# Queries of 16 of 32 head groups by seven products of quarters, and one buffer for query weights, in a float32 decoder kernel

## The chip, the cores and the metric

The kernel runs on one core of one Trainium2 chip. The metric is the device time of one execution in microseconds (us). Three runs of the kernel before took 1465.74 us in the median (1463.15 to 1471.24). The engines of the core are named as in the profile: PE multiplies matrices, PEld is its loading of weights, DVE and ACT work elementwise and along rows, POOL does some elementwise work and the indexed DMAs, SP issues DMAs. All data are float32.

## The reference: what is computed

Four batches of 512 rows of 512 values (x) go through two gated layers. Layer 0 is a small self-attention over a context and a linear layer whose weights are made of bits. Layer 1 is a cross-attention of 16 heads and a mixture of 16 experts, which works on batch 0 alone. The part that the change touches is the query of layer 1:

```python
q = (hidden_states @ Wq).reshape(B, Sq, H, D)      # 512 wide in, 16 heads of 128
k = (encoder_hidden_states @ Wk).reshape(B, Skv, H, D)
v = (encoder_hidden_states @ Wv).reshape(B, Skv, H, D)
q = rmsnorm(q, gq)
k = rmsnorm(k, gk)
scores = jnp.einsum('bqhd,bkhd->bhqk', q, k) * scale
attn = jax.nn.softmax(scores, axis=-1)
out = jnp.einsum('bhqk,bkhd->bqhd', attn, v)
return out.reshape(B, Sq, H * D) @ Wo
```

## The kernel before

**Groups and steps.** Layer 1 works in 32 groups: batch b (4) by pair of heads g (8), `groups[m]`. One step is one head, i = 0 to 63, with m, h = divmod(i, 2); h is 0 in an even step and 1 in an odd one. `step(i)` (L1187) issues four quarters. Each starts with one tile of scores (L856: 128 queries by 512 keys, into one of two psS banks), followed by pieces of other work so that PE always has something to do.

**What lies in a step.** In an even step: keys and values of the next group (`keys_values`, L733, eight matmuls of 512 columns, two quarters), then the values product of the head two steps back (`values`, L903, third quarter), then half of the output projection of the group two back (`project`, L954, fourth quarter). In an odd step: the queries of the next group (`queries`, L807, one head in the first quarter and one in the second), `values`, and the other half of a projection.

**Queries.** `queries(m, h)` multiplies the 128 columns of the weights of head h by `lx1[b]`, the normalised and transposed rows of the batch, in four matmuls of 512 columns into one of three psA banks. ACT squares the result into `sq` (L813) and copies it, scaled, into `qT` (L815). After the second head, `part` on DVE sums the squares in blocks (L827), `total` on PE adds over partitions (L835), and `scale` makes 1/rms on DVE (L840 to L843) and POOL (the power at L192). The exponential of the scores needs it.

**Scores to probabilities.** For each tile of scores: DVE takes the maximum (L864) and multiplies it (L866), ACT takes the exponential (L873), DVE divides (L877, L878) and transposes blocks (L260). After a head's fourth tile SP moves the blocks across partitions with 16 DMAs (L268, `big<-tP`), into one of two buffers that `values` reads.

**The keys' way.** POOL scales the keys (L759), DVE transposes blocks (L770), and ACT issues one DMA out and four back (L777, L785, `kT<-k_d`).

**Order.** All work is issued in an order written out by hand: `tick()` counts matmuls, `later(n, f)` issues f when n more were counted, and `put(i, quarter, f)` adds f to a quarter of a step. Engines run their instructions in that order.

**Weights.** `load_wq` (L708), `load_wkv` (L142) and `load_wo` (L714) are issued by SP. Each has two buffers. `load_wq(m + 2)` is issued in the second quarter of the even step of group m.

**Experts.** From step 22 to step 55, 17 blocks of 128 gathered rows take two steps each: transposes (L1021), two products of 352 columns (`hidden`, L1029), the gate on ACT and DVE (L1038, L1039, L1043), transposes (L1048), a product down (`down`, L1057), a copy to `y` (L1065) and its DMA out. From step 57 on, 16 gathers on POOL (L1104) bring these rows back and DVE adds them to x (L275), four a step, each ten ticks after its gather. Four times in the kernel the rows of a batch are normalised and transposed for the queries (`turned_rows`, L226, L244, L249).

Of the kernel before, what the change touches and what calls it, by code (L numbers as in the profile page):

```python
# [9 lines left out]
F32 = mybir.dt.float32  # L10
# [21 lines left out]
FCH = [(0, 128), (128, 128), (256, 96)]  # L32
NSLOT = 2 * NE - 1
SPILL = 1
TB = 32
# [19 lines left out]
def tile_gated_decoder(  # L55
# [31 lines left out]
    def ps_a():  # L87
        return ps("psA", 3)
# [16 lines left out]
    def row(tag, bufs):  # L105
        return work.tile([P, 512], F32, tag=tag, bufs=bufs, name=tag)

    def col(n, tag):
        return tiny.tile([P, n], F32, tag=tag, name=tag)

# [95 lines left out]
    def rows_stats(b):  # L206

        stats = {}

        def chunk(c):  # L210
            if c == 0:
                stats["mv"] = tiny.tile([P, NC, 2], F32, tag="mv", name="mv")
            st = col(6, "st")
            nc.vector.bn_stats(st, x_sb[:, b * NC + c, :])
            nc.vector.bn_aggr(stats["mv"][:, c, :], st)
            if c == NC - 1:
                ve = col(NC, "ve")
                nc.vector.tensor_scalar(ve, stats["mv"][:, :, 1], EPS, None, ALU.add)
                stats["rs"] = col(NC, "rs")
                rsqrt(stats["rs"], ve, NC)  # L220

        return [lambda c=c: chunk(c) for c in range(NC)], stats

    def normalised(b, c, mv, rs):
        xn = row("xn", 2)
        nc.vector.tensor_scalar(  # L226
            xn, x_sb[:, b * NC + c, :], mv[:, c, 0:1], rs[:, c : c + 1], ALU.subtract, ALU.mult
        )
        return xn
# [96 lines left out]
    def l0_stats(b):  # L326

        pieces, stats = rows_stats(b)

        def gates():  # L330
            gate0[b] = gr = col(NC, "gr")
            nc.vector.tensor_scalar(gr, stats["rs"], tg[:, 0:1], None, ALU.mult)
            gm = col(NC, "gm")
            nc.vector.scalar_tensor_tensor(gm, stats["mv"][:, :, 0], -1.0, gr, ALU.mult, ALU.mult)
            for c in range(NC):
                x_c = x_sb[:, b * NC + c, :]
                later(c, lambda x_c=x_c, c=c: nc.scalar.activation(
                    x_c, x_c, AF.Identity, bias=gm[:, c : c + 1]
                ))

        return pieces[:-1] + [lambda: (pieces[-1](), later(3, gates))]
# [75 lines left out]
    def layer0_attention():  # L417
# [57 lines left out]

        load_wq(0)
        load_wq(1)
        load_wo(0)
# [15 lines left out]
        for h in range(G):  # L494
            queries(0, h)
        linear(NB - 1, turned0[NB - 1], [0, 1])

# [19 lines left out]
    def route():  # L517
# [20 lines left out]

        zero = row("xg", 1)
        nc.gpsimd.memset(zero, 0.0)  # L540
# [10 lines left out]
        ef_b = ef.unsqueeze(1).broadcast_to(CE)  # L551
        hit = small_tile([P, TOPK, NC, NE], "hit")
        for k in range(TOPK):
# [103 lines left out]
    def bias_row():  # L657
# [23 lines left out]
        yield  # L681
        brow.append(row("y", 2))
        nc.vector.tensor_copy(brow[0], pb)
# [17 lines left out]
    wq_of, wo_of = {}, {}  # L701
    q_of, sq_of, rq_of, kn_of, k_of, v_of, o_of = {}, {}, {}, {}, {}, {}, {}
    turned, moved, ends = {}, {}, {}
    n_heads = G * len(groups)

    def load_wq(m):
        t = work.tile([P, KC, GD], F32, tag="wq", name="wq")
        nc.sync.dma_start(t, wq_v[:, :, cols(m)])  # L708
        wq_of[m] = t

# [6 lines left out]
    def keys_values(m, chunks):  # L717
# [32 lines left out]
        def scale():  # L750
            kss = col(NC * G, "kss")
            nc.vector.tensor_reduce(
                kss, st["sq"].rearrange("p c (h d) -> p (c h) d", h=G), AX.X, ALU.add
            )
            nc.vector.tensor_scalar(kss, kss, 1.0 / D, EPS, ALU.mult, ALU.add)
            rk = col(NC * G, "rk")
            rsqrt(rk, kss, NC * G)
            kn_v = kn.rearrange("p c (h d) -> p c h d", h=G)
            nc.gpsimd.tensor_tensor(  # L759
                kn_v, kn_v,  # L760
                rk.rearrange("p (c h) -> p c h", h=G).unsqueeze(3).broadcast_to([P, NC, G, D]),
                ALU.mult,
            )
# [33 lines left out]
    def queries(m, h):  # L797
# [21 lines left out]
        if h < G - 1:  # L819
            return  # L820
        n = G * S // TB
        st = {}

        def part():

            st["part"] = col(n, "part")
            nc.vector.tensor_reduce(  # L827
                st["part"], sq.rearrange("p h (j r) -> p (h j) r", r=TB), AX.X, ALU.add,
                apply_transpose=True,
            )  # L830
# [6 lines left out]
        def scale():  # L837

            own = col(n, "own")
            nc.vector.tensor_tensor(own, st["pq"][:, 0:n], mine, ALU.mult)  # L840
            v = col(G * NC, "qss")
            nc.vector.tensor_reduce(v, own.rearrange("p (c a) -> p c a", a=NT), AX.X, ALU.add)
            nc.vector.tensor_scalar(v, v, 1.0 / D, EPS, ALU.mult, ALU.add)  # L843
            rq_of[m] = col(G * NC, "rq")
            rsqrt(rq_of[m], v, G * NC)
# [319 lines left out]
    for c in range(NC):  # L1165
        for k in range(TOPK):
            put(last + 1 + c, k, lambda c=c, k=k: add_row(c, k))
    for b in range(1, NB):
        i = (b - 1) * NG * G + NG
        for j, f in enumerate(turned_rows(b, lx1, lnt)):  # L1170
            put(i + j // NC * (1 + j % NC), 3 if j >= NC else j, f)
        if b > 1:
            put(i, 3, lambda b=b: load_ctx(b))
# [13 lines left out]
    def step(i):  # L1187
        m, h = divmod(i, G)
        pieces = [[], [], [], []]
        if i >= G:  # L1190
            pieces[0 if i == n - 1 else 2].append(lambda: values(i - G))
        elif h > 0:
            pieces[3].append(lambda: tick(8))
        if i == n - 1:
# [7 lines left out]
        if h == 0:  # L1202
            if 0 < m < M - 1:
                pieces[0].append(lambda: keys_values(m + 1, [0, 1]))
                pieces[1].append(lambda: keys_values(m + 1, [2, 3]))
            if m + 2 < M:
                pieces[1].append(lambda: load_wq(m + 2))
                pieces[3].append(lambda: load_wkv(m + 2))
            if m >= 2:
                pieces[3].append(lambda: project(m - 2, [2, 3]))  # L1210
            if 2 <= m < M:
                pieces[3].append(lambda: later(4, lambda: load_wo(m)))
        elif i < n - 1:
            if m + 1 < M:
                pieces[0].append(lambda: queries(m + 1, 0))
                pieces[1].append(lambda: queries(m + 1, 1))
            if m >= 1:
                pieces[3].append(lambda: project(m - 1, [0, 1] if m < M else [0, 1, 2, 3]))
        for quarter in range(4):
            if i < n:  # L1220
                scores(i, quarter)
            for f in pieces[quarter] + extra.get((i, quarter), []):
                f()
# [73 lines left out]
```

## Time and profile before

| what | value |
|---|---|
| median of three runs | 1465.74 us |
| the profiled execution's own time | 1464.92 us |
| its span, first to last instruction | 1462.8 us |
| granted PE clock, mean | 0.993 |
| scores L856 on PE | 262.7 us, 512 instructions |
| keys and values L733 on PE | 231.9 us, 512 |
| queries L807 on PE | 231.3 us, 512 |
| values L903 on PE | 226.6 us, 504 |
| projection L954 on PE, three kinds of bank | 124.9 + 66.2 + 60.1 us |
| experts' hidden products L1029 on PE | 86.0 us, 272 |
| idle of PE before the projection, for ACT's oT (L910) | 11.0 us |

The page gives for each engine the time in which it was busy. Matmuls overlap, so a group's busy time over its count is not what one costs in a row; start to start is. Idle time of an engine counts only where another one waits for it: the views of waits name who ended a wait. Windows cut the span into stretches, since shares of the whole mix stages with different limits.

### The profile page before, as it was taken

The page shows a single profiled execution, that of the slowest core. Times are in us where ns is not written, and L with a number is a line of the kernel's source. Part 1 is how long each engine was busy: PE and PEld are TensorE (multiplying, and loading weights), DVE is VectorE, ACT ScalarE, POOL GpSimd, SP SyncE. Part 2 cuts the span into 40 slices and gives each one's busy share as a digit, 9 for nine tenths or more (in the row PEclk, how much of TensorE's full clock was granted, in tenths as well). Part 3 has the DMA queues.
Part 4 walks back from the last instruction along what each step waited for, and adds up shares of the span by engine and source line. Part 5 has one row for each costly group of instructions (what it writes and reads, how often), then busy time and mean ns, then how long its engine had stood idle before and what let it go on. Part 6 is the DMA issues. An engine that isn't in the chain of part 4 may idle for free.

```text
span 1462.8 us, 13699 instructions
## 1 busy us (share of the span) xinstructions
PE 1427.7 (98%) x3745; PEld 669.5 (46%) x3745; DVE 962.3 (66%) x2160; ACT 533.4 (36%) x1196; POOL 286.2 (20%) x210
## 2 busy tenths in 40 slices
PE   8999999999999999999999999999999999999898
PEld 4544444444444444444444444444444444444334
DVE  4778766677776776665655565665666556567784
ACT  4642233333443433334233333323433333333331
POOL 1324415323111111111111111111011111102310
PEclk9999999999999999999999999999999999999999
DMA  7424016545544545566556576556556656545642
GB/s 258 168 96 163 1 55 164 149 139 128 138 133 132 143 134 166 157 184 169 176 177 178 159 214 192 145 172 204 170 162 186 183 168 192 167 135 167 180 128 74
DMA packets 155346, 226.89 MB, mean 155 GB/s; under 512 B 24576, under 2 KB 90640, under 8 KB 155264
## 3 DMA queue, kind: packets, MB, share of 16 engines
q1 hardware_dynamic: 127312, 177.86, 41.7%
q10 hardware_dynamic: 23040, 33.56, 7.5%
q0 software_dynamic: 4912, 14.53, 3.5%
q8 instruction: 33, 0.54, 0.2%
q14 instruction: 49, 0.40, 0.1%
HBM read 129.62 MB, written 30.17 MB: 109 GB/s over the span
## 4 chain that ended last, share of the span: by engine, by line
PE 79%; DVE 10%; SPq 4%; ACT 3%; DMA 2%; issue 1%; POOL 0%; ACTq 0%; DVEq 0%; POOLq 0%
PE psA L733 13%; PE psS L856 12%; PE psA L807 12%; PE psO L903 11%; PE psA L954 6%; PE psA L1029 6%; PE psO L954 4%; SPq L268 4%; PE psT L954 3%; PE psA L1057 3%; PE psA L363 2%; DMA big<-tP 2%; ACT prob L873 2%; DVE tP L260 1%; PE psA L691 1%; DVE nmax L864 1%
## 5 line engine op out<-in xcount | busy, mean ns | idle before, releaser
L873 ACT ACTIVATE prob<-psS,sb,rq 128x512 f32<-128x512 f32 x256 | 199.2, 778 | 607.0 <-DVE sb L866 605.5
L856 PE MATMUL psS<-kT,qT 128*128 128x512 f32 x512 | 262.7, 596 | 2.2 <-ACT prob L873 1.1
L733 PE MATMUL psA<-wkv,ctx 128*128 128x512 f32 x512 | 231.9, 592 | 0.0
L807 PE MATMUL psA<-lnT,wq 128*128 128x512 f32 x512 | 231.3, 592 | 0.0
L903 PE MATMUL psO<-big,v 128*128 128x512 f32 x504 | 226.6, 592 | 0.0
L864 DVE TENSOR_REDUCE nmax<-psS 128x1 f32<-128x512 f32 x256 | 172.7, 675 | 30.7 <-PE psS L856 28.9
L877 DVE RECIPROCAL rden<-den 128x1 f32<-128x1 f32 x256 | 40.7, 159 | 224.5 <-ACT prob L873 223.2
L260 DVE STREAM_TRANSPOSE tP<-prob 128x512 f32<-128x512 f32 x252 | 179.1, 711 | 8.4 <-DVE prob L878 0.5
L807 PEld LDWEIGHTS psA<-lnT,wq 128*128 128x128 f32 x512 | 96.7, 190 | 118.6 <-issue 108.1
L903 PEld LDWEIGHTS psO<-big,v 128*128 128x128 f32 x504 | 95.8, 190 | 120.5 <-issue 112.6
L733 PEld LDWEIGHTS psA<-wkv,ctx 128*128 128x128 f32 x512 | 96.4, 190 | 118.8 <-issue 112.3
L192 POOL TENSOR_TENSOR rq<-qss,mhalf 128x8 f32<-128x8 f32 x32 | 53.2, 1661 | 493.5 <-DVE qss L843 493.4
L192 POOL TENSOR_TENSOR rk<-kss,mhalf 128x8 f32<-128x8 f32 x32 | 52.6, 1644 | 443.3 <-DVE rden L877 281.4
L878 DVE TENSOR_SCALAR prob<-prob,rden 128x512 f32<-128x512 f32 x256 | 133.1, 520 | 9.0
L954 PE MATMUL psA<-wo,oT 128*128 128x512 f32 x256 | 124.9, 606 | 11.1 <-ACT oT L910 11.0
L856 PEld LDWEIGHTS psS<-kT,qT 128*128 128x128 f32 x512 | 93.4, 191 | 91.6 <-issue 71.4
L1029 PE MATMUL psA<-gu,xgT 128*128 128x352 f32 x272 | 86.0, 459 | 0.0
L954 PEld LDWEIGHTS psA<-wo,oT 128*128 128x128 f32 x256 | 48.3, 192 | 74.5 <-issue 55.5
L770 DVE STREAM_TRANSPOSE tK<-kn 128x256 f32<-128x256 f32 x128 | 45.4, 412 | 39.1 <-POOL kn L759 39.1
L1029 PEld LDWEIGHTS psA<-gu,xgT 128*128 128x128 f32 x272 | 51.7, 190 | 37.9 <-issue 16.3
L954 PE MATMUL psO<-wo,oT 128*128 128x512 f32 x128 | 66.2, 643 | 0.0
L275 DVE SCALAR_TENSOR_TENSOR x_sb<-psA,tg,x_sb 128x512 f32<-128x512 f32 x80 | 57.9, 724 | 6.7 <-PE psA L691 3.8
(173 smaller groups left out, 1509.4 us busy)
## 6 DMA issues: line engine op xcount, KB each, us to landing
big<-tP SPq DMA_DIRECT2D x1008, 64.0 KB
k_d<-tK ACTq DMA_DIRECT2D x32, 512.0 KB
kT<-k_d ACTq DMA_DIRECT2D x128, 128.0 KB
wq<-in_wq_dram SPq DMA_DIRECT2D x32, 512.0 KB
wo<-in_wo_dram SPq DMA_DIRECT2D x32, 512.0 KB
gu<-in_gate_dram SPq DMA_DIRECT2D x16, 704.0 KB
gu<-in_up_dram SPq DMA_DIRECT2D x16, 704.0 KB
wkv<-in_wk_dram SPq DMA_DIRECT2D x32, 256.0 KB
```

The costliest lines, as they stand in the source:

```text
L192: nc.gpsimd.tensor_tensor(out, v, mhalf[:, :n], ALU.pow)
L260: nc.vector.transpose(tP[:, :, c, :], e.rearrange("p (j r) -> p j r", r=TB))
L268: nc.sync.dma_start(pT[t * TB : (t + 1) * TB, g].rearrange("r j q -> r (j q)"), tP[g * TB : (g + 1) * TB, t * NC : (t + 1) * NC].rearrange ...
L733: nc.tensor.matmul(pp, ctxs[b][:, k, c * P : (c + 1) * P], wkv[:, k, :, :].rearrange("p a n -> p (a n)"), start=(k == 0), stop=(k == CC - 1),)
L807: nc.tensor.matmul(pp, wq[:, k, h * D : (h + 1) * D], lx1[b][:, k, :], start=(k == 0), stop=(k == KC - 1))
L856: nc.tensor.matmul(sc, q_of[m][h][:, c * P : (c + 1) * P], k_of[m][:, :, h, :], start=True, stop=True)
L864: nc.vector.tensor_reduce(nmax, sc, AX.X, ALU.max, negate=True)
L873: nc.scalar.activation(e, x, AF.Exp, bias=sb, scale=scale, accum_out=st["den"])
L878: nc.vector.tensor_scalar(st["e"], st["e"], rden, None, ALU.mult)
L903: nc.tensor.matmul(po, v[:, k, h * D : (h + 1) * D], pT[:, :, k, :], start=(k == 0), stop=(k == NC - 1))
L954: nc.tensor.matmul(pp, oT[:, j, c * P : (c + 1) * P], wo[:, j, :], start=(j == 0), stop=(j == G - 1))
L1029: nc.tensor.matmul(st[a][:, :FF], st["xgT"][:, k * P : (k + 1) * P], st["gu"][:, a, k, :], start=(k == 0), stop=(k == KC - 1),)
```

## The change

For groups 12 to 27 (`SWITCH`) the queries of a group, a product of 256 weight columns (two heads) by 512 rows with 512 summed over, are cut into quarters: heads by halves of the sum by halves of the rows. Seven products of quarters, each two matmuls of 256 columns, take the place of eight such products (which are the eight matmuls of 512 columns). The sums and differences of quarters that they need are made by POOL for the weights (`combine`), once for each group, by DVE for the rows (`combine_rows`), once for each of three batches, and by ACT and DVE for the results (`second`, `fourth`, `upper`, `lower`). Four products are issued in the last quarter of the even step (part 0) and three in the second quarter of the odd step (part 1). They stay in two psA banks in between.

```diff
     def load_wq(m):
-        t = work.tile([P, KC, GD], F32, tag="wq", name="wq")
-        nc.sync.dma_start(t, wq_v[:, :, cols(m)])
-        wq_of[m] = t
+        w = work.tile([P, KC, GD], F32, tag="wq", bufs=1, name="wq")
+        nc.sync.dma_start(w, wq_v[:, :, cols(m)])
+        if not by_quarters(m):
+            wq_of[m] = w
+            return lambda: None
...
+        def combine():
+            s1, s2, s4 = (sums[:, j] for j in range(3))
+            s3 = quarter(1, 0)
+            nc.gpsimd.tensor_tensor(s1, quarter(1, 0), quarter(1, 1), ALU.add)
+            nc.gpsimd.tensor_tensor(s2, s1, quarter(0, 0), ALU.subtract)
+            nc.gpsimd.tensor_tensor(s3, quarter(0, 0), s3, ALU.subtract)
+            nc.gpsimd.tensor_tensor(s4, quarter(0, 1), s2, ALU.subtract)
+            wq_of[m] = [quarter(0, 0), quarter(0, 1), s4, quarter(1, 1), s1, s2, s3]
+
+        return combine
+
+    def combine_rows(b):
...
+        nc.vector.tensor_tensor(t3, quarter(1, 1), quarter(0, 1), ALU.subtract)
+        nc.vector.tensor_tensor(t1, quarter(0, 1), quarter(0, 0), ALU.subtract)
+        nc.vector.tensor_tensor(t2, quarter(1, 1), t1, ALU.subtract)
+        nc.vector.tensor_tensor(t4, quarter(1, 0), t2, ALU.subtract)
+        lxs_of[b] = [quarter(0, 0), quarter(1, 0), quarter(1, 1), t4, t1, t2, t3]
...
+    def quarter_queries(m, part):
+        ws, xs = wq_of[m], lxs_of[groups[m][0]]
+
+        def product(j, out, start):
+            for k in range(HK):
+                nc.tensor.matmul(
+                    out, ws[j][:, k, :], xs[j][:, k, :], start=start and k == 0, stop=k == HK - 1,
+                    skip_group_check=True,
+                )
+                tick(0.5)
+
+        if part == 0:
+            px, py = ps_a(), ps_a()
+            q_of[m] = q0, q1 = [row("qT", 3) for h in range(G)]
...
+            def second():
+                nc.scalar.copy(u2, px[:, 0:HS])
+                nc.vector.tensor_tensor(u2, px[:, HS:S], u2, ALU.add)
+
+            def fourth():
+                nc.vector.tensor_tensor(u3, py[:, 0:HS], u2, ALU.add)
+                nc.vector.tensor_tensor(q1[:, HS:S], py[:, HS:S], u3, ALU.add)
+
+            product(0, px[:, 0:HS], True)
+            product(5, px[:, HS:S], False)
+            later(0, second)
+            product(6, py[:, 0:HS], True)
+            product(4, py[:, HS:S], False)
+            later(0, fourth)
+            return
...
+        def upper():
+            nc.scalar.copy(q0[:, 0:HS], px[:, 0:HS])
+            nc.vector.tensor_tensor(q1[:, 0:HS], px[:, HS:S], u3, ALU.add)
+
+        def lower():
+            nc.vector.tensor_tensor(q0[:, HS:S], py[:, HS:S], u2, ALU.add)
+            for h in (1, 0):
+                nc.scalar.activation(sq[:, h, :], q_of[m][h], AF.Square)
+            for h in (0, 1):
+                nc.scalar.activation(q_of[m][h], q_of[m][h], AF.Identity, scale=gqk)
+
+        product(1, px[:, 0:HS], False)
+        product(3, px[:, HS:S], True)
+        later(0, upper)
+        product(2, py[:, HS:S], False)
+        later(0, lower)
+        square_sums(m, sq)
```

`square_sums` holds the old `part`, `total` and `scale` unchanged. In `step` (q is m + 1, late says that group q is made by quarters):

```diff
-            pieces[0 if i == n - 1 else 2].append(lambda: values(i - G))
+            pieces[0 if i == n - 1 or h and late else 2].append(lambda: values(i - G))
...
             if m + 2 < M:
-                pieces[1].append(lambda: load_wq(m + 2))
-                pieces[3].append(lambda: load_wkv(m + 2))
-            if m >= 2:
+                pieces[2 if late else 3].append(lambda: load_wkv(m + 2))
+            if m >= 2 and not late_before:
                 pieces[3].append(lambda: project(m - 2, [2, 3]))
...
+            if late and q < M:
+                pieces[3].append(lambda: quarter_queries(q, 0))
         elif i < n - 1:
...
+            if q < M:
+                pieces[1].append(lambda: (quarter_queries if late else queries)(q, 1))
+            if m + 2 < M:
+                pieces[2].append(lambda: later(6, load_wq(m + 2)))
+            if late:
+                pieces[2].append(lambda: project(m - 1, [0, 1]))
             if m >= 1:
-                pieces[3].append(lambda: project(m - 1, [0, 1] if m < M else [0, 1, 2, 3]))
+                pieces[3].append(lambda: project(m - 1, [2, 3] if late else [0, 1]))
+            if late and q < M:
+                pieces[3].append(lambda: later(2, lambda: load_wo(q)))
...
-            for f in pieces[quarter] + extra.get((i, quarter), []):
+            more = extra.get((i, quarter), [])
+            for f in more + pieces[quarter] if late and h and quarter == 2 else pieces[quarter] + more:
```

In words: in odd steps before a changed group the values product comes in the first quarter, both halves of a projection in the third and fourth, and the load of the next `wo` after them. For all groups the query weights are loaded in the third quarter of the odd step instead of the second of the even one, into the one buffer; before the first step, `load_wq(1)` is issued after the queries of group 0.

The rest makes room for `wqs` and `lxs`: most of the small column tiles get two or three buffers instead of eight, the normalised rows `xn` share the two buffers of `y`, `zero` uses the buffer of `xgT`, `brow` that of `xg`, and `hit` that of `tK`. And the 16 row additions at the end are spread three to a step:

```diff
-            put(last + 1 + c, k, lambda c=c, k=k: add_row(c, k))
+            put(last + 1 + (c * TOPK + k) // 3, (c * TOPK + k) % 3, lambda c=c, k=k: add_row(c, k))
     for b in range(1, NB):
...
+        if (b + 1) * NG > SWITCH[0]:
+            put(2 * max(b * NG, SWITCH[0]) - 2, 1, lambda b=b: combine_rows(b))
```

## The prediction

> **What bounds the kernel now.** First the page's engine table and its row of tenths, then the windows by stage, the waits of PE, and the timeline of one group amid the expert blocks.
>
> ```profile
> PE 1427.7 (98%) x3745; PEld 669.5 (46%) x3745; DVE 962.3 (66%) x2160; ACT 533.4 (36%) x1196; POOL 286.2 (20%) x210
> ```
>
> PE is busy for 98% of the span, but a busy PE need not be a paced one. The windows show where it is full (columns: stretch, length, then busy time and instructions of PE, PEld, DVE, ACT, POOL, the granted clock, DMA share, GB/s):
>
> ```profile
> 178.00:581.00 403.00, 396.20 (x947) 176.34 (x946) 285.98 (x628) 152.98 (x351) 90.42 (x65) 0.99 0.48 132
> ...
> 780.00:980.00 200.00, 200.00 (x524) 95.41 (x523) 120.21 (x273) 70.09 (x163) 30.16 (x19) 1.00 0.61 180
> ...
> 1300.00:1463.00 163.00, 148.55 (x376) 67.58 (x374) 110.48 (x229) 50.78 (x118) 31.26 (x25) 0.97 0.48 136
> ```
>
> From 581 to 1300 us, where the 17 expert blocks and the 16 changed groups lie, PE has no idle time and the waits of PE list nothing; DVE is busy 60%, ACT 35%, DMA 61%. So in that stretch time is what PE streams, and a microsecond less of matmul is a microsecond less of span as long as nothing else becomes late. The timeline gives the rate (start, length, engine, line, tiles, shape, count):
>
> ```profile
> 623.76 2.53 PE L1029 MATMUL psA<-gu,xgT 128*128 128x352 f32 x8
> 626.13 1.02 PE L856 MATMUL psS<-kT,qT 128*128 128x512 f32 x2
> ...
> 637.94 3.60 PE L807 MATMUL psA<-lnT,wq 128*128 128x512 f32 x8
> 641.37 0.49 PE L1048 MATMUL psT<-ident,hh 128*128 128x128 f32 x3
> ```
>
> ```profile
> 1444.98 1.06 PE L934 MATMUL psA<-big,v 128*128 128x128 f32 x8
> 1445.87 0.60 PE L924 MATMUL psT<-ident,prob 128*128 128x128 f32 x4
> ```
>
> Lengths contain an overlapping tail, so I read from start to start. Each matmul of the program is two instructions (x8 for four). 512 columns: (641.37-637.94)/8 = 0.429 us. 352 columns: (626.13-623.76)/8 = 0.296. 128 columns: (1445.87-1444.98)/8 = 0.111. Cost is proportional to columns, with hardly a fixed part: 0.84 ns a column above.
>
> **PE: removed and added.** A changed group drops 2 heads x 4 matmuls = 16 instructions of 512 columns (L807): 16 x 0.429 = 6.87 us. It adds 7 products x 2 matmuls x 2 = 28 instructions of 256 columns. The trace has no 256-column matmul. Between the 128 and 352 rows a line gives 0.217, from 352 and 512 downward 0.216; bounds by the nearest rows are 0.111 and 0.296. I take 0.216: three points lie on one line. The weight loads (0.19 us each, L807) now come every 0.216 us instead of 0.429; the 128-column row has the same load and still issues every 0.111, so loads hide behind one another. 28 x 0.216 = 6.05. Gain: 0.82 us a group, 16 groups: **-13.1 us**. By the bounds: 28 x 0.111 = 3.11 (-60 us) and 28 x 0.296 = 8.29 (+23 us); both contradict the line, so I keep them as remote.
>
> The Trainium skill speaks against the change here: "TensorE: Matmul & The Clock Gate", section "Back-to-back issue gap", has sustained spacings of about 81 ns at 128 columns and 131 ns at 512, so a matmul of a quarter of the columns costs 62% of a full one. A line through its two figures makes 256 columns 75% of 512, hence 28 x 0.75 against 16, an estimate of 30% more query time, some +33 us in all. This trace has 26% (0.111 to 0.429) where the page has 62%, so the measurement decides.
>
> **Other engines, per changed group** (42.6 us, 594.4 to 637.1; none of this is on PE, so it is free while PE's waits stay empty):
> - DVE gains 5 adds of 128x256 with a PSUM operand. Bounds: 0.16 us (128x1, L866) and 0.74 (128x512, L275); nearest are 128x352 at 0.48 (L1043) and the 128x256 transposes at 0.41; I take 0.40, 2.0 us. Three times DVE also makes 4 sums of rows, 128x512 from SBUF: 0.49 to 0.74 each (L878, L275), 2 to 3 us, two quarters ahead of their use.
> - ACT loses 2 squares (0.60) and 2 scaled copies (0.69) from PSUM, and gains the same four from SBUF and 2 copies of 128x256 (0.37 each, L727): +0.75 us.
> - POOL gains 4 sums of 128x256. kn (L759) does 128x1024 in 1.90: 0.48 each by size, at most 1.90 each; I take 0.5, 2.0 us. While such an instruction runs, DVE can stand still: one sb (L866, normally 0.16) took 1.86 us from 1352.99, beside the kn that ran 1352.94 to 1354.84. So up to 2 us of DVE a group.
> - DVE thus goes from 26 to at most 30 of 42 us. psS has two buffers: the exponential has to end before the scores two quarters on. Today the tightest such margin amid blocks is 3.9 us (third quarter of an odd head, 645.99 after an exp that ended 642.1), others 5 to 10. The shorter query quarters take about 0.85 us off it and the added work a few tenths: still covered.
> - DMA moves the same bytes. The query weights (512 KB) now have one buffer: their load may start only after the previous group's products, in the third quarter of the odd head. SP issues the 16 moves of the head before until then (head 33: until 11.2 us after its start, the products ending at 8.1), so its wait is over when its turn comes and no move queues behind it. A load takes 3.4 to 6.7 us from issue to its last signal. POOL's sums wait for it; behind them on POOL stands the rsqrt of the next keys, some 15 us on, and the sums' use comes about as late. At the start wq of group 1 may load once the queries of group 0 end at 186.8, and is needed at 204.9. Covered; uncovered, the load's 3.4 to 6.7 us would stand in every group.
> - The value products of odd heads move from the third to the first quarter, 9 us earlier. Their transposed probabilities land about 20 us ahead of use today (head 33: last move 839.4, landed 841.4, used 861.8); 11 stay. Two of three psA banks stay taken from the even head's last quarter to the odd head's second; between, nothing else asks for psA. The second half of the products waits for the sums that empty these banks; PE comes 7 us after the first half (0.86 of products, then 4.6 of scores, values and transposes, 0.86 of scores, 0.86 of products), they need under 2. Behind that wait on PE stand the next scores.
>
> **What is late next.** The sum of squares (L827 on DVE, then L835 on PE). Head 33, start 809.38:
>
> ```profile
> 813.82 2.25 ACTq L785 DMA_DIRECT2D kT<-k_d  x2
> ...
> 817.60 0.78 ACT L873 ACTIVATE prob<-psS,sb,rq 128x512 f32<-128x512 f32 x1
> ...
> 820.63 1.24 DVE L827 TRANSPOSE_TENSOR_REDUCE part<-sq 128x32 f32<-128x1024 f32 x1
> ...
> 825.17 0.30 PE L835 MATMUL psT<-part,same 128*128 128x32 f32 x2
> ```
>
> ACT stands in the kT issues till 816.1 (6.7 after the head's start), where a landing of `big<-tP` ends its wait; L827 ends 821.9 and L835 runs 3.3 us later. After the change, from 6.7: copies of oT and hT 1.2, exp 1.0, DVE's share 0.65, upper add 0.4, transpose 0.7, lower add 0.4, both squares 1.2, L827 1.24: 13.5, with hand-overs 13.7. PE arrives at 4.63 (scores, values, hh) + 3.45 (scores, three products) + 0.86 + 2.58 + 3.44 = 14.96. A margin of 1.2 instead of 3.3. Where ACT leaves kT at 8.0 to 8.6 (heads 25, 27, 29, 41, 43, 45, some with an lnT copy besides), it is gone: L835 waits 0 to 1 us there. Six times 0.5: **+3 us** (0 to 6). Behind L835 on PE stand the next scores, so this is lost time.
>
> **Tail.** The 16 row additions go from four to three a step, over six steps. PE now idles 1.2 at 1361, 3.5 at 1368 and 2.1 at 1408 us, in steps where DVE has these additions (0.71 each) besides ACT's wait for DMA. One addition less in step 59, one to three more in steps 61 and 62: **-0.5**, between -4 and +3. The rest (fewer small buffers, xn in y's buffers, zero and brow elsewhere) has the same readers some tens of us away: 0.
>
> **Sum.** -13.1 + 3 - 0.5 = -10.6 against the profiled execution's own 1464.92 (span 1462.8 and 2.1 around it): 1454.3, say **1454 us**. Its time lies 0.8 below the median of 1465.74, within the runs' spread (1463.15 to 1471.24).
>
> **Rivals.**
> - The late sum of squares in every changed group. For it: the margin is only 1.2, and POOL's weight sums can hold DVE up to 2 us. Against: those sums are queued behind the rsqrt that L835 itself feeds. At 1 us in each of 16 groups instead of 3 in all: -13.1 + 16 - 0.5 = +2.4, 1467; half of that 1459.
> - Slower: 256-column instructions don't keep the column rate, weight loads being the limit. Place: the 28 instructions of each group. It decides from 6.87/28 = 0.245 us each; at the 352-column price 0.296 it is +22.6 us, 1487. Against it: the 128-column row at 0.111.
> - The score buffers stop covering: DVE's and ACT's added 2 to 5 us a group fall ahead of an exponential in the odd head's third quarter, where the margin is 3.9 - 0.85 = 3.0. For it: POOL's hold on DVE. Against it: the additions lie in other quarters. It decides from 0.66 us beyond that in each of 16 groups; at 2 us: -10.6 + 32 = +21, 1486.
> - The margin holds everywhere and the tail gains 4: -13.1 - 4 = 1448.
>
> **Chances.** Forecast (1450 to 1458) 0.66; late sums of squares in all groups 0.16, of which 0.04 still below 1458; column rate lost 0.04; score buffers 0.05; margin and tail both better 0.09. A measurement of this kernel can tell about 0.5% (7.3 us) from no change, so faster means below 1458.4: 0.66 + 0.04 + 0.09 = 0.79; within: 0.12; slower: 0.09. Slower is the column rate and the score buffers. The range takes in the better tail at 1448 and the margin lost in most groups, up to 1463 (about 0.75 us in each of 16); beyond it lie some 0.15. The remote bounds of the 256-column price are outside.
>
> **What would show it.** Right: query products from start to start 0.216 us each, a changed group 41.8 instead of 42.6 us, PE full from 581 to about 1290, waits of PE there only L835 on L827, some 3 us. Wrong: spacing above 0.245; waits of scores (L856) on the exponential, or of products on the added sums; SP waiting for PE in the wq load with moves behind it.

## The result and the profile after

The changed kernel takes 1461.75 us (median of 20 runs, 1459.21 to 1465.72) against 1468.66 for the kernel before in 20 runs beside it (1463.15 to 1472.85; three of them had given the 1465.74 shown above). The ratio is 0.9961, 95% interval 0.995 to 0.9971: 4 to 7 us faster, where I had forecast 10.6 less than the profiled execution. That is within the 0.5% that counts as no change, to which I gave 0.12; the time itself lies inside the range (1448 to 1463). The profiled execution took 1460.5 us (span 1458.8).

The engine row of the page, and then the windows (busy time and instructions of PE, PEld, DVE, ACT, POOL, then granted clock, DMA share, GB/s):

```profile
PE 1415.0 (97%) x3937; PEld 705.7 (48%) x3937; DVE 996.2 (68%) x2252; ACT 544.4 (37%) x1228; POOL 333.2 (23%) x274
```

```profile
178.00:581.00 403.00, 395.52 (x960) 176.65 (x959) 287.00 (x629) 153.81 (x354) 94.52 (x70) 1.00 0.48 133
581.00:1300.00 719.00, 713.17 (x2101) 382.01 (x2100) 477.24 (x1084) 268.97 (x632) 150.66 (x129) 1.00 0.59 177
780.00:980.00 200.00, 200.00 (x587) 107.42 (x586) 132.19 (x304) 75.93 (x177) 44.54 (x39) 1.00 0.61 182
1300.00:1459.00 159.00, 142.93 (x363) 65.08 (x361) 106.41 (x221) 48.81 (x113) 31.33 (x25) 0.98 0.48 137
```

PE's work fell by 12.7 us (1427.7 to 1415.0) and the span by only 4.0. Amid the expert blocks PE now stands idle for 719.00 - 713.17 = 5.8 us; before, it stood for none. From 780 to 980 it is still full. The waits of PE from 581 to 1300 us name the two places (us, times, longest):

```profile
PE psT L245 <- DVE y L227: 3.5, 4, 1.0
PE psA L1160 <- ACT hT L1153: 2.3, 2, 1.2
```

L245 are the transposes of the next row block's normalised rows (`xn`, L227, in a buffer of `y`), L1160 the `down` product of an expert block, which needs `hT`. The wait that I forecast, L938 (the sum of squares) on L930, isn't there.

The product instructions, from start to start, run at the forecast rate:

```profile
594.85 1.03 PE L872 MATMUL psA<-lnT,wq 128*128 128x256 f32 x4
595.71 1.03 PE L872 MATMUL psA<-lxs,wqs 128*128 128x256 f32 x4
596.58 1.03 PE L872 MATMUL psA<-lxs,wq 128*128 128x256 f32 x4
```

(596.58 - 594.85)/8 = 0.216 us for 256 columns. Counting from the first score of one even head to the next, an ordinary changed group takes 41.82 us in place of 42.64. But six groups, those that begin at heads 24, 26, 28 and 40, 42, 44 and in which the next block's rows are normalised and transposed, take 43.25, 43.90, 43.69 and 43.21, 43.90, 43.70, together 261.64; they took 259.34 before. At 0.82 less each they would take 254.4. So **7.2 us are lost in these six groups**; the view of waits, which counts from the modelled ends of matmuls, shows 5.8 of them as idle PE.

How, in head 25 (start 640.12). ACT first:

```profile
644.12 0.89 ACTq L827 DMA_DIRECT2D kT<-k_d  x2
...
645.32 4.59 ACTq L827 DMA_DIRECT2D kT<-k_d  x2
649.95 0.37 ACT L1153 COPY hT<-psT 128x256 f32<-128x256 f32 x1 [5.05 <-DMA big<-tP]
...
650.85 0.79 ACT L976 ACTIVATE prob<-psS,sb,rq 128x512 f32<-128x512 f32 x1
```

ACT issues the four reads of the keys amid SP's 16 moves (641.49 to 653.40); the third and fourth issue take 4.59 us, and it is free 9.8 us after the head's start (8.1 in the kernel before). PE reaches `down` at 649.20, because `step` now puts the expert's work first in the third quarter and the query products are shorter; `hT` is copied only from 649.95, and PE waits 1.17 us. In the kernel before, PE came to `down` 13.2 us after the head's start, now after 9.1. PE after the change, in heads 25 and 26:

```profile
650.37 2.85 PE L1160 MATMUL psA<-dn,hT 128*128 128x512 f32 x6 [1.17 <-ACT hT L1153]
...
664.73 0.66 PE L245 MATMUL psT<-ident,y 128*128 128x128 f32 x4 [0.98 <-DVE y L227]
```

The same places in the kernel before, where head 25 starts at 637.08 and head 26 at 657.38 (ACT's reads, PE's `down`, DVE's `xn`):

```profile
642.30 2.90 ACTq L785 DMA_DIRECT2D kT<-k_d  x2
...
650.28 2.74 PE L1057 MATMUL psA<-dn,hT 128*128 128x512 f32 x6
...
658.12 0.53 DVE L226 TENSOR_SCALAR xn<-x_sb,mv,rs 128x512 f32<-128x512 f32 x1
```

DVE after the change:

```profile
651.77 0.16 DVE L980 RECIPROCAL rden<-den 128x1 f32<-128x1 f32 x1 [4.63 <-ACT prob L976]
...
659.69 0.74 DVE L276 SCALAR_TENSOR_TENSOR x_sb<-psO,tg,x_sb 128x512 f32<-128x512 f32 x1
...
663.51 0.71 DVE L276 SCALAR_TENSOR_TENSOR x_sb<-psT,tg,x_sb 128x512 f32<-128x512 f32 x1
664.14 0.53 DVE L227 TENSOR_SCALAR y<-x_sb,mv,rs 128x512 f32<-128x512 f32 x1
```

It idles 4.63 us for that exponential, and everything behind is late. All four adds of the projection (L276) now fall in or behind the odd head, three of them ahead of `xn`, which starts 3.13 us into head 26; before it started 0.74 us into it. PE wants it at 663.75 and starts the transposes at 664.73. So late a stop of ACT is found in two heads only, 25 and 41. In heads 27 and 43 it is free after 7.3 and 7.4 us, sooner than before (8.0), and still PE waits for `xn` in heads 28 and 44, again with three of the four adds ahead of it.

The counterpart of the group shown before, head 33 (start 812.77):

```profile
817.41 2.28 ACTq L827 DMA_DIRECT2D kT<-k_d  x2
...
820.63 0.79 ACT L976 ACTIVATE prob<-psS,sb,rq 128x512 f32<-128x512 f32 x1
...
824.25 1.25 DVE L930 TRANSPOSE_TENSOR_REDUCE part<-sq 128x32 f32<-128x1024 f32 x1
...
827.71 0.30 PE L938 MATMUL psT<-part,same 128*128 128x32 f32 x2
```

PE comes to L938 14.94 us after the start (14.96 was worked out); L930 ends at 12.7 and not 13.7, a margin of 2.2 us.

Every kernel below can be held against one stretch: from the first score of head 22 to that of head 56, which has all 16 groups. It takes 728.35 us before and 722.43 after, 5.92 less, about what the medians say. Outside it, profiles differ by some us either way with the place of short stretches in which the granted clock is 0.50 (the last section), so I read the stretch first and the medians second. The stretch has a spread of its own: kernels that differ only after it are 1.4 us apart (the changed kernel and e1_tail4) or 1.2 (e9 and e11), while three profiles without a wait in it (e7, e13, e14) agree to 0.01.

### The profile page after: what moved, and what is told of

It is laid out like the page before. It is cut to its first block, busy times and chain, and to the rows that moved or that the text cites. A ratio compares the mean times of both kernels' runs of the same rounds, so it can differ in the third digit from the quotient of the medians.

```text
span 1458.8 us, 14422 instructions
## 1 busy us (share of the span) xinstructions
PE 1415.0 (97%) x3937; PEld 705.7 (48%) x3937; DVE 996.2 (68%) x2252; ACT 544.4 (37%) x1228; POOL 333.2 (23%) x274
## 4 chain that ended last, share of the span: by engine, by line
PE 74%; DVE 13%; ACT 4%; SPq 3%; DMA 3%; POOL 1%; issue 1%; ACTq 0%; POOLq 0%; DVEq 0%
PE psA L775 14%; PE psS L959 11%; PE psO L1006 11%; PE psA L1057 6%; PE psA L872 5%; PE psA L849 5%; PE psA L1132 5%; PE psO L1057 3%; SPq L269 3%; PE psT L1057 3%; PE psA L364 2%; PE psA L1160 2%; ACT prob L976 2%; DMA big<-tP 2%; DVE tP L261 2%; DVE x_sb L276 2%
## 5 line engine op out<-in xcount | busy, mean ns | idle before, releaser
L1057 PE MATMUL psA<-wo,oT 128*128 128x512 f32 x256 | 121.9, 595 | 12.0 <-ACT oT L1013 12.0
L849 PE MATMUL psA<-lnT,wq 128*128 128x512 f32 x256 | 115.6, 592 | 0.0
L849 PEld LDWEIGHTS psA<-lnT,wq 128*128 128x128 f32 x256 | 48.3, 190 | 59.3 <-issue 52.6
L276 DVE SCALAR_TENSOR_TENSOR x_sb<-psA,tg,x_sb 128x512 f32<-128x512 f32 x80 | 58.2, 727 | 6.7 <-PE psA L694 3.8
```

The costliest lines, as they stand in the source:

```text
L276: nc.vector.scalar_tensor_tensor(x_sb[:, t, :], src, gate, x_sb[:, t, :], ALU.mult, ALU.add)
L849: nc.tensor.matmul(pp, wq[:, k, h * D : (h + 1) * D], lx1[b][:, k, :], start=(k == 0), stop=(k == KC - 1))
L1057: nc.tensor.matmul(pp, oT[:, j, c * P : (c + 1) * P], wo[:, j, :], start=(j == 0), stop=(j == G - 1))
```

## The experiments

**Theory A**: ACT's stop in the key reads, amid SP's moves, makes those heads late. **Theory B**: VectorE has too many adds in the odd heads, ahead of what PE waits for. Further suspects: buffers now shared or single, and the row additions at the end. The kernel before was run beside every kernel; ratios are to it.

**e2_no_quarters**: no group by products, everything else of the change kept.

```diff
-SWITCH = (12, 28)
+SWITCH = (99, 99)
```

> The changed kernel with an empty range of changed groups: all queries by four matmuls of 512 columns in the old order; the single weight buffer, the smaller and shared buffers and the spread of the row additions stay. Theory: these cost nothing but the end, about 2.5 us, ratio 1.002. Rival: single and shared buffers cost time of their own, 5 us or more, ratio 1.005 and above, with waits for query weights or for y in the profile.

Measured 1466.77 us, ratio 1.0001 (0.9989 to 1.0013), not the 1.002 expected; the stretch takes 728.36 us, to 0.01 that of before. So single and shared buffers, the load order and the fewer small tiles cost nothing by themselves; loss and gain belong to the products and the order that comes with them.

**e1_tail4**: the row additions four to a step again.

```diff
-            put(last + 1 + (c * TOPK + k) // 3, (c * TOPK + k) % 3, lambda c=c, k=k: add_row(c, k))
+            put(last + 1 + c, k, lambda c=c, k=k: add_row(c, k))
```

> The changed kernel with its 16 row additions put back to four a step (steps 57 to 60). Theory: of the expected gain some 2.5 us were given back at the end: three additions fall into step 62, which is short, DVE is late with the maximum, PE waits 4.1 us for an exponential there and runs 3.4 us at half clock after it; against that the spread saves about 2 us before. So this runs about 2.5 us faster than the changed kernel, ratio to before about 0.994, and the 4.1 us wait is gone. Rival: the wait moves to steps 59 and 61 and the time stays, 0.996.

Measured 1457.18 us, ratio 0.993 (0.9917 to 0.9944), and the wait of 4.1 us for an exponential in step 62 is gone, though one of 2.8 us for a move (`big<-tP`) stands there instead. I took this for the price of that edit; e12 to e14 below show that it isn't. e5 to e10 and e14 carry this edit too; e2, e3, e4, e11 and e13 leave the row additions as the change has them.

**e3_xn_early**: the changed kernel with `xn` normalised two quarters earlier, ahead of the projection's adds.

```diff
-            put(i + j // NC * (1 + j % NC), 3 if j >= NC else j, f)
+            put(i + j // NC * (1 + j % NC), (1 if b > 1 else 3) if j >= NC else j, f)
```

> The changed kernel with the normalised rows of batches 2 and 3 made by DVE in the second quarter of a step instead of the fourth. Theory: in the six groups with row transposes 7.2 us are lost, of which 3.5 us because DVE comes late to the normalised row at the end of the odd head, behind four additions of a projection that now all fall into that head; in the second quarter DVE has time, so the waits of PE on these rows go and the time falls by 3 to 4 us, ratio about 0.9935. Rival: DVE is late everywhere in these groups (added sums, POOL's hold on it); then the wait appears at another place and the time stays, 0.996.

Measured 1461.32 us, ratio 0.9959 (0.9943 to 0.9975): no gain that can be told. The groups from heads 26, 28, 42 and 44 came down to 42.69 and 42.25, but those from 24 and 40 rose to 44.77 and 44.48, with PE again waiting for `xn` (3.1 us) behind an exponential that stood behind ACT's key reads. The six groups take 259.13 us, 2.5 less: part of the loss is gone, part moved from four groups into two, and its source stayed.

**e4_keys_late**: the key reads four ticks later in the changed groups.

```diff
-        later(18, take_in)
+        later(22 if by_quarters(m) else 18, take_in)
```

> The changed kernel with the four DMAs that bring the transposed keys back (kT) issued by ACT four ticks later in changed groups, behind the copies of hT and oT. Theory: PE's waits of 2.3 us for hT come from ACT standing in these issues; ACT then copies hT at once, the waits go, and the margin of the sum of squares stays: 2 to 3 us faster than the changed kernel, ratio about 0.9945. Rival: ACT stands as long, only later, and the sum of squares (the matmul that adds over partitions) waits instead: no gain or a loss of some us, 0.996 to 0.999.

Measured 1471.59 us, ratio 1.0033 (1.002 to 1.0046): slower than both. The waits of PE, 581 to 1300 us:

```profile
PE psA L1057 <- DVE qT L906: 6.7, 14, 1.1
PE psT L245 <- DVE y L227: 5.9, 4, 1.7
```

Now nearly every changed group waits, for the psA bank that the upper add empties: ACT stops later, the exponential and the copy in front of that add with it. The expectation had the sum of squares late as the rival; the bank is what waits. When ACT stops matters.

**e5_keys_sp** and **e6_keys_pool**: ACT issues no key reads at all; SP does in e5 (the diff), GpSimd in e6.

```diff
-                nc.scalar.dma_start(
+                nc.sync.dma_start(
                     kT[j * TB : (j + 1) * TB].rearrange("r t h q -> r t (h q)"),
```

> The changed kernel with the row additions four to a step again (as e1_tail4) and with the four reads that bring the transposed keys back (kT<-k_d, L827) issued by SP in place of ACT; nothing else. Theory A (the loss in the six groups that make row transposes comes from ACT standing in those four issues, until 9.8 us after the head's start, behind SP's own moves): ACT is free some 4 us earlier, exp, hT's copy and the adds follow, the groups from heads 24, 26, 28, 40, 42 and 44 fall from 43.2 to 43.9 us to about 41.9 to 42.7 us, together some 5 to 7 us less than e1_tail4: about 1451 us, ratio to the kernel before 0.988 to 0.990. Theory B (VectorE has too many adds in the odd heads, and ACT's stop is only a symptom): these groups keep over 43 us and the time stays at e1_tail4's 1457 us, ratio 0.993. Third way: SP's queue, now four issues longer, brings the loads behind the moves late, and weights or y rows are waited for: over 1460 us, with waits on wq, gu or y in the trace.

Measured 1523.87 us, ratio 1.0394 (1.0359 to 1.0429): the third way. Behind SP's moves the keys come too late all over the kernel (PE, whole span):

```profile
PE psS L959 <- DMA kT<-k_d: 65.3, 28, 7.9
```

> As e5_keys_sp, but the four reads of the keys go by GpSimd's queue, which holds no moves. Theory A: as there, 1451 us, ratio 0.988 to 0.990, the same six groups at 41.9 to 42.7 us. Theory B: 1457 us, ratio 0.993. Third way: GpSimd's own sums of the query weights and its scaling of the keys (kn, L801) come late behind the issues: groups of the zone that were 41.82 us go over it, slower than 1457 us.

Measured 1462.17 us, ratio 0.996 (0.9946 to 0.9974). But from 588 to 1300 us PE waits for nothing, the six groups take 254.40 us and the others 41.81: the whole 7.2 us are back with all four adds still in the odd head. The time is spent elsewhere, once, in heads 20 to 23 (GpSimd):

```profile
574.31 1.09 POOL L1112 DMA_INDIRECT xg<-xn_d,rowi  x1 [14.42 <-DMA xn_d<-y]
576.44 2.24 POOL L827 DMA_DIRECT2D kT<-k_d  x4 [1.04 <-PE psO L1057]
```

The first gather of expert rows holds GpSimd's queue until `xn` is written, the key reads stand behind it, and the next scores wait 7.2 us, once, with the granted clock at 0.50 for 10.2 us about it. Without ACT's stop, then, there is no loss in the six groups: ACT's stop is needed for it.

**e7_two_adds_back**: half of each projection (two adds) back in the even head, where the kernel before has it.

```diff
-            if m >= 2 and not late_before:
+            if m >= 2:
                 pieces[3].append(lambda: project(m - 2, [2, 3]))
...
-                pieces[2].append(lambda: project(m - 1, [0, 1]))
+                pieces[2].append(lambda: project(m - 1, [0]))
...
-                pieces[3].append(lambda: project(m - 1, [2, 3] if late else [0, 1]))
-            if late and q < M:
-                pieces[3].append(lambda: later(2, lambda: load_wo(q)))
+                pieces[3].append(lambda: project(m - 1, [1] if late else [0, 1]))
```

> The changed kernel with the row additions four to a step again, and with half of each projection (two of its four chunks, two adds of VectorE) put back into the even head's last quarter, where the kernel before has it, so that the odd head has two adds (some 1 us of VectorE) and 1.7 us of TensorE less in its second half. Keys are still read by ACT. Theory B (adds crowd the odd heads): the six groups with row transposes lose less, 2 to 4 us off e1_tail4's time, ratio 0.990 to 0.992. Theory A: ACT's stop stays, the row transposes and hT are waited for as before, and hT has less TensorE work ahead of it or the same: 1457 us or up to 2 us more, ratio 0.993 to 0.995.

Measured 1454.96 us, ratio 0.9911 (0.9888 to 0.9934). PE waits for nothing from 581 to 1300 us, the six groups take 254.40 us, and the stretch takes 715.19, 13.17 less than before. (Half a projection is 3.44 us of PE, not the 1.7 of the expectation.) The timeline of ACT shows why this isn't yet theory B:

```profile
641.71 4.05 ACTq L827 DMA_DIRECT2D kT<-k_d  x4
645.81 0.78 ACT L976 ACTIVATE prob<-psS,sb,rq 128x512 f32<-128x512 f32 x1 [3.81 <-DMA big<-tP]
```

Head 25 starts at 643.15 here. ACT still stops 4 us, but from 1.4 us before the head until 2.6 us into it, not until 9.8 (9.0 in e1_tail4): the projection's ticks in the even head had also moved the key reads ahead of the odd head's first exponential. Two experiments try to separate the two effects.

**e9_keys_soon**: the adds stay, the reads alone go ahead of that exponential.

```diff
-        later(18, take_in)
+        later(16 if by_quarters(m) else 18, take_in)
```

> The changed kernel with the row additions four to a step again and, in groups 12 to 27, the four reads of the keys (kT<-k_d) due 16 ticks after the keys in place of 18, so that in ACT's order they stand ahead of the odd head's first exp, not behind it, and go out with SP's first moves and not amid them. All four adds of the projection stay in the odd head. Theory A (it is ACT's stop in these issues, amid SP's moves, that makes the six groups long): ACT leaves them about 4 us earlier than in e1_tail4 (9.0 us after the start of head 25 there), the six groups fall to 41.8 to 42.7 us, ratio to the kernel before 0.989 to 0.992. Theory B (four adds of VectorE in the odd head are too many): the six groups stay over 42.4 to 43.9 us, ratio 0.993. Third way: ACT now stands for the landing of the keys' writing (2.6 us) ahead of an exp, and every changed group is longer than 41.82 us: ratio 0.995 or more.

Measured 1463.66 us, ratio 0.9961 (0.9945 to 0.9976); the stretch 724.80, worse than in e1_tail4 (721.03). The six groups take 261.47, and four others (from heads 30, 32, 46 and 52) now go over 41.82 as well, the third way in part. ACT in head 25, start 644.20:

```profile
646.21 4.64 ACTq L827 DMA_DIRECT2D kT<-k_d  x4
650.90 0.78 ACT L976 ACTIVATE prob<-psS,sb,rq 128x512 f32<-128x512 f32 x1 [6.28 <-DMA big<-tP]
```

ACT leaves the reads at 6.7 us, but now the first exponential is what stands behind them, 6.28 us. My simple cure from theory A was wrong: the reads cost some 4 us of ACT here as in e7 (3.2 to 5.4 in heads 23 to 53 here, 4.05 to 4.7 there). What e7 has and this kernel has not is reads that are over 2.6 us into the odd head, and two adds fewer.

**e10_adds_back_keys_late**: e7 with `later(22 if by_quarters(m) else 18, take_in)`, so that the reads stand behind that exponential again.

> e7_two_adds_back (two adds of the projection back in the even head) with the reads of the keys due 22 ticks after the keys in place of 18 in groups 12 to 27, which puts them behind the odd head's first exp again, as in the changed kernel; in e7 the added ticks had put them ahead of it. Theory A: with ACT's stop back, the six groups with row transposes are long again, by 3 to 7 us together, ratio 0.993 to 0.997. Theory B: with two adds fewer in the odd head they stay at 41.8 and 42.7 us as in e7, ratio 0.991.

Measured 1456.13 us, ratio 0.9918 (0.9897 to 0.994). e7 had no wait of PE from 581 to 1300 us; here one is back:

```profile
PE psT L245 <- DVE y L227: 2.5, 3, 1.0
```

The six groups take 257.55 us, a loss of 3.1 against e7's none, 5.8 in e1_tail4 and the changed kernel's 7.2; ACT leaves the reads up to 7.4 us into the head. So with two adds fewer, reads that stand inside the odd head cost about half of the loss. It takes ACT's stop inside the odd head; that the adds of the moved projection make it about twice as dear fits these numbers, but is not shown by itself, since ACT also leaves sooner here (7.4 us at the latest, against 9.0 and 9.8).

**e8_wide**: groups 8 to 11 by products too.

```diff
-SWITCH = (12, 28)
+SWITCH = (8, 28)
```

> The changed kernel with the row additions four to a step again, and with the products of quarters in 20 groups in place of 16: groups 8 to 11 as well, which have no expert block beside them (34.56 us each). If TensorE bounds those groups as it does the others and nothing new is waited for, each gives another 0.82 us: 3.3 us less than e1_tail4, ratio 0.991. If without an expert block there is too little TensorE work to cover the adds, the exps and the copies behind them, these four groups stay at 34.6 us or go over it: 1457 to 1465 us, ratio 0.993 to 0.998.

Measured 1471.2 us, ratio 1.0016 (0.9999 to 1.0033). The four stretches from heads 14, 16, 18 and 20, which make these groups' queries beside no expert block, take 37.17, 37.77, 40.83 and 41.52 us, where the changed kernel has 34.56 three times and 36.58. The waits of PE from 400 to 600 us begin:

```profile
PE psT L938 <- DVE part L930: 7.4, 3, 3.1
PE psA L775 <- DVE x_sb L276: 2.4, 3, 1.6
```

In these groups stands the wait that I had forecast; no block's matmuls lie ahead of L938 there.

**e11_keys_soon_rows3**: e9 with the row additions three to a step.

> The changed kernel with the reads of the keys at 16 ticks as in e9_keys_soon and nothing else: the row additions stay three to a step. Beside e9_keys_soon it prices the edit of the row additions alone. If that edit costs what e1_tail4 and the changed kernel differ by (4.5 us, with a wait of 4.1 us on the exp in step 62): e9's time and 2 to 5 us. If the difference was the place of the half-clock intervals and not the edit: e9's time, within 1 us.

Measured 1463.6 us, ratio 0.9973 (0.9959 to 0.9986): e9's median within 0.1 us. That speaks against what I had taken from e1_tail4; e12, and e13 against e14, test it.

**e12_before_rows3**: the kernel before with the row additions three to a step and nothing else.

> The kernel before with one edit of the change alone: the row additions three to a step. If that edit costs what e1_tail4 and the changed kernel differ by: 3 to 5 us slower than the kernel before, ratio 1.002 to 1.0035. If it costs nothing, as e9_keys_soon and e11_keys_soon_rows3 have it: ratio 0.999 to 1.001.

Measured 1468.43 us, ratio 1.0005 (0.999 to 1.0019).

**e13_adds_back_rows3**: the changed kernel with e7's diff alone; **e14_adds_back_again**: e7 unchanged.

> e7_two_adds_back with the row additions three to a step, as the changed kernel has them: the changed kernel with nothing but half of each projection back in the even head. Its zone is free of waits, as e7's, so it prices the edit of the row additions again, and the projection's move by itself. If the additions cost 4.5 us: 1459 to 1460 us, ratio 0.994. If they cost nothing: e14's time within 1 us, ratio 0.991.

> e7_two_adds_back once more, unchanged, as the partner of e13_adds_back_rows3 on the same chip and as a second measurement of the best kernel so far: ratio to the kernel before 0.991 (0.9888 to 0.9934 the first time), with the groups of the zone at 41.81 and 42.69 us.

Measured 1455.38 and 1454.03 us, both with ratio 0.9908 (0.9891 to 0.9926), stretch 715.18 in both. The row additions cost nothing that can be measured. What separates e1_tail4 from the changed kernel beyond its 1.4 us in the stretch stays open.

The ledger: the stretch against the kernel before (us), and the median of the kernel against that of the runs of before beside it.

| kernel | stretch, heads 22 to 56 | median |
|---|---|---|
| e2_no_quarters | 0.0 | -1.2 |
| e12_before_rows3 | 0.0 | -0.2 |
| changed kernel | -5.9 | -6.9 |
| e1_tail4 | -7.3 | -10.7 |
| e3_xn_early | -8.4 | -6.6 |
| e4_keys_late | +4.5 | +3.7 |
| e5_keys_sp | +25.4 | +56.7 |
| e6_keys_pool | -10.2 | -5.0 |
| e8_wide | -11.3 | +4.0 |
| e9_keys_soon | -3.6 | -3.2 |
| e11_keys_soon_rows3 | -4.8 | -3.3 |
| e10_adds_back_keys_late | -10.0 | -10.7 |
| e7, e13, e14 | -13.2 | -12.2, -13.3, -14.6 |

In e8 half a projection (3.44 us) lies ahead of the stretch, and so do the four added groups that lose time. e13 is the changed kernel with one part of its new order undone, and beats both kernels by about 0.5% and 0.9%.

## Why the prediction was right or wrong

- **PE, -13.1**: right. 0.216 us an instruction, 0.82 a group, and e7, e13 and e14 show all 16 x 0.82 = 13.2 in the stretch. The rule on spacing that I weighed ("TensorE: Matmul & The Clock Gate" of the Trainium skill, "Back-to-back issue gap") would have made these groups longer; 0.216 measured against 0.429 at 512 columns decides against it here.
- **Late next, +3**: the step that failed. I followed only one consumer behind ACT, the sum of squares, and bounded the loss at 6. It is late nowhere amid the blocks: in heads 25 and 41 L930 ends 15.6 us after the start, and PE, itself held by `hT`, comes at 16.4. Two others were nearer. `hT`: my own sum has PE at `down` after 4.63 + 3.45 + 0.86 = 8.94 us (9.08 measured in head 25, 13.2 before), and I never held that against ACT, which I had leaving the reads at 8.0 to 8.6 there (it was 9.8). And `xn`, behind adds moved into the odd head. The loss was 7.2 (5.8 in e1_tail4). The six groups that I named did pay, but not as I had it: ACT leaves the reads late in heads 25 and 41 alone, and in heads 27, 29, 43 and 45 at 6.9 to 7.4 us, sooner than before (8.0 to 8.4). All of it is gone in e6, where ACT issues no reads, and in e7, where the reads are over early in the head and two adds are back.
- **Other engines "free while PE's waits stay empty"**: true on average (DVE busy 66% from 581 to 1300 us), and the wrong question. I counted DVE's added work but gave no position to the projection adds that only moved; they stand in front of `xn`.
- **The buffers, the load, the value products**: covered, as costed (e2, and e7 without a wait). GpSimd's sums, 0.73 us each where I took 0.5, are in e6 and e7 too, so a hold of DVE by them does not make the loss by itself.
- **Tail, -0.5**: not told from nothing (e12, e13 against e14).
- **Sum**: -13.1 + 7.2 = -5.9 is the stretch of the changed kernel. I took the profiled execution as the level, 1464.92; the median of 20 runs is 3.7 higher. So the time misses 1454.3 by 7.4: half of it is that level, half a gain of 6.9 in place of 10.6. That it still lies inside the range is luck: the range reached 1463 for a sum of squares late in most groups, which no group shows.
- **Rivals**: the column rate held. No score waits for an exponential amid the blocks. The sum of squares is waited for in no changed group of this kernel, but is in e8.

## What to carry to other kernels

When an edit moves work, list for each engine in order what now stands in front of every instruction that the bottleneck waits for, moved instructions as well as new ones, and redo all the margins of that stretch, not only the tightest of before. An engine that also issues transfers may have to wait in them for another queue's transfers to land, as ACT does here: place such issues where nothing urgent stands behind them. A gain that holds in most groups and fails in a few is found by timing group by group; the share of busy time showed nothing.

## What the runs showed of the hardware

- Four key reads took ACT 3.4 to 5.8 us in heads 23 to 53 of the changed kernel, 66.1 us in 16 stops. The issues themselves are 25.6 of that (0.31 us at the shortest); 39.9 are 30 waits between them. The trace's records name the semaphore (the counter that tells of a landing) of each transfer: SP and ACT share eight of them, and each of the 30 waits ended when one of SP's moves landed on the semaphore that the read was to use next. For the last read of head 25 (SP's move, ACT's read):

```profile
644.59 0.59 SPq L269 DMA_DIRECT2D big<-tP  x1
```

```profile
649.60 0.31 ACTq L827 DMA_DIRECT2D kT<-k_d  x1
```

  That move landed at 649.58. GpSimd's transfers use eight other semaphores, and in e6 its four reads took 2.3 us with no wait between them. Reads by ACT with semaphores of their own were not tried. The Trainium skill ("Perfetto Trace Analysis", "DMA Instruction — HWDGE (DVE, Sync)") says that the issuing engines share one descriptor generator and that its lock is part of the recorded time; by the records such a lock could lie in the 25.6 us of the issues, not in the 39.9 between them.
- The granted clock goes to 0.50 for 3.41 us at a time, or multiples, after some of PE's pauses (not after one of 2.8 us that ended at 1404.6): in the changed kernel from 1366.1 and from 1413.9, the second after the 4.1 us wait in step 62. A stretch of 3.41 us costs some 1.7 us of PE's time, by half the clock, and the profiles above have them in different places; a difference of a few us outside the expert blocks shouldn't be read as the edit's. "TensorE: Matmul & The Clock Gate" of the Trainium skill ("What's actually happening") has half rate after an idle window of about 3.4 us; the 3.41 us measured agrees with it.
- GpSimd's sums of 128x256 took 0.72 to 0.93 us, mostly 0.73, not the 0.5 that I scaled from 1.90 us at 128x1024: their time does not go by size alone. VectorE's adds of 128x256 took 0.38 to 0.42 (0.40 was taken).
